# Layer 1 of a four-layer graph network: the scatters of the attention weights in bursts of two and of three, three and two

## The chip, the core and the metric

The kernel runs on one core of a Trainium2 chip. The core has a matrix engine (TensorE, PE in the profile, with its weight loads as PEld), a vector engine (VectorE, DVE), an activation engine (ScalarE, ACT), a general engine (GpSimd, POOL) and SyncE (SP), which here issues most DMA transfers. Each engine runs its own instructions in their order; semaphores hold an instruction until others are done. Scatters with computed rows are DMA transfers that GpSimd issues. The metric is the device time of one execution in microseconds.

## The reference

The input x is 128 graphs of 64 nodes with 256 features, 8192 tokens in all. Four layers follow, each on h = relu(layernorm(x)), each added to x. Layer 1, in which the change lies, is attention over a list of 512 edges:

```python
Xq = (H @ W_lin.T).reshape(bt, n, h, dh)
Xv = (H @ W_val.T).reshape(bt, n, h, dh)
e = einsum('behd,hd->beh', leaky_relu(Xq[:, src] + Xq[:, dst], 0.2), a)
e = e + log(A0[src, dst] + EPS)[None, :, None]
# softmax of e over the edges with the same src: segment_max, exp, segment_sum, division
Y = segment_sum(attn[..., None] * Xv[:, dst], src)
return Y.reshape(bt, n, d) @ W_out.T
```

Layer 0 is two graph convolutions with windows of an LSTM, layer 2 two linear maps with batch normalisation around an aggregation, layer 3 a dense graph attention.

## The kernel before

Tokens go in 16 chunks of 512, and four chunks make a group (0 to 3). Layer 1 has two phases that overlap.

The first is `edges(q)`, 32 times, two blocks of 128 tokens each: queries and values by `project` (L1090), a product that gathers source and target of each edge (L1119), the activation (L1125), the join (L1131), the score of eight blocks gathered in one bank (L1140), at the group's end the linear part (L1156). On GpSimd beside it stand the head sums (L1107), and the roots (L106 to L109) and placed rows (L130) of the next chunks' layer norm. When a group's scores are complete, `edge_softmax(g)` is put on the list `behind`. It is a generator: each `yield` is a place at which it stops, and `step_behind()` takes it one place on. `edges` calls it three times per q, so a group has 24 steps before the next group's scores come. Its steps are the exponent's argument (L1165), two scans for the segment maximum (L1168, L1170), subtraction and exponent (L1174, L1175), two scans for the sum (L1178, L1180), four reciprocals (L1185), a product (L1187), four transposes (L1193), the copy into `attn` (L1208, in the last group L1201 on ScalarE), and eight scatters (L1222). Each scatter writes 128 rows of 64 numbers into a field in HBM, whose other entries are zero; `come_back` (L1247) then loads that field, 2 MB, as the dense attention `dense[g]`.

The second phase is `values_of(n)`, once per chunk: `weigh(n)` has 64 small products of values and attention (L1320, the "small products") and one copy to SBUF (L1330, yT); then comes what `behind` has to do, the loads for chunk n + 2 (values L1272, residual L1293), `turn_attention` (L1302, two att copies from dense, on ScalarE and VectorE), the store of an earlier chunk (L1425), and `put_out` of the chunk before (L1342, the output product, and two additions L1352 that release its PSUM banks). Last come `sums`, the layer-norm statistics for layer 2 (L1362, L1365 on VectorE; x_rs and x_nm, L1367 to L1372, on GpSimd). Sums of chunks 2 to 5 are held and paid from chunk 7 on, two per chunk. Chunks 0 to 3 run within the last eight `edges`, chunks 4 to 15 behind them.

The last group's scores are ready at chunk 3. Its softmax runs beside chunks 3 to 6 and must give `dense[3]` for chunk 12 (`LAST`). In this group each scatter also waits for the last small product issued so far (`last_weigh`, by `add_manual_dep`), and `come_back` is issued within chunk 9. In the kernel before, chunk 6 takes it through the transposes and `attn`, and chunk 7 calls `finish_behind()`, which issues all eight scatters behind chunk 7's small products, so its `yield` after five scatters has no effect.

The order of instructions on an engine follows the program, except where a scheduler may move one; `late(...)` marks those that it must keep in program order. The PSUM banks are a ring of four (`bank`) and of two pairs (`pair`).

Of the kernel before, what the change touches and what calls it, by code (L numbers as in the profile page):

```python
# [31 lines left out]
def gnn_stack_kernel(ctx: ExitStack, tc: tile.TileContext, a: dict, out: bass.AP):  # L32
# [3 lines left out]
    NGR = NTOK // GROUP  # L36
# [7 lines left out]
    def bank():  # L44
        return psums["now"].tile([P, 512], F32, tag="bank", name="bank", bufs=psums["banks"])
# [32 lines left out]
    def late(ins):  # L78

        tc.keep_in_program_order(ins)  # L80
# [398 lines left out]
    with ExitStack() as l0:  # L479
# [451 lines left out]
        for slot in range(len(tasks) + 2):  # L931
# [26 lines left out]
            if new:  # L958
# [8 lines left out]
                if step.w == MAX_SKIP and step.t == 2 and k < 2 and step.g < NGR - 1:  # L967
                    for u in range(2):
                        n = 4 * step.g + 2 * u + k
                        later.append((slot, "x", n))  # L970
            while later and later[0][0] <= slot:
                _, kind, n = later.pop(0)
# [27 lines left out]
    with ExitStack() as l1:  # L1000
# [32 lines left out]
        for g, c, u, ip in last_outs:  # L1033
            if not ip:
                n = 4 * g + 2 * u + c
# [126 lines left out]
        def edge_softmax(g):  # L1162

            e = e1.tile([P, E], F32, tag="e", name="e")
            late(nc.vector.scalar_tensor_tensor(e, scores[g], 0.8, logw, ALU.mult, ALU.add))  # L1165
            run = e1.tile([P, E], F32, tag="run", name="run")
            yield
            late(nc.vector.tensor_tensor_scan(run, first, e, NEG, ALU.add, ALU.max))  # L1168
            yield
            late(nc.vector.tensor_tensor_scan(  # L1170
                run[:, ::-1], final[:, ::-1], run[:, ::-1], NEG, ALU.add, ALU.max
            ))
            yield
            late(nc.vector.tensor_tensor(e, e, run, ALU.subtract))  # L1174
            late(nc.scalar.activation(e, e, AF.Exp))  # L1175
            yield

            late(nc.vector.tensor_tensor_scan(run, keep, e, 0.0, ALU.mult, ALU.add))  # L1178
            yield
            late(nc.vector.tensor_tensor_scan(  # L1180
                run[:, ::-1], final[:, ::-1], run[:, ::-1], NEG, ALU.add, ALU.max
            ))
            yield
            for k in range(NE):
                late(nc.vector.reciprocal(run[:, k * P : (k + 1) * P], run[:, k * P : (k + 1) * P]))  # L1185
                yield
            late(nc.vector.tensor_tensor(e, e, run, ALU.mult))  # L1187
            yield
            for _ in range(2 if g < NGR - 1 else 0):
                yield  # L1190
            p = bank()
            for ec in range(NE):
                ins = nc.tensor.transpose(p[:, ec * P : (ec + 1) * P], e[:, ec * P : (ec + 1) * P], ident)  # L1193
                if ec == 0:
                    late(ins)
            if g < NGR - 1:
                yield
            attn = e1.tile([P, E], F32, tag="run", name="attn").rearrange("p (e r) -> p e r", e=NE)
            if g == NGR - 1:
                for ec in range(NE):  # L1200
                    late(nc.scalar.activation(  # L1201
                        attn[:, ec, :],
                        p[:, ec * P : (ec + 1) * P],
                        AF.Identity,
                        scale=twins[:, ec : ec + 1],
                    ))
            else:
                late(nc.vector.tensor_tensor(  # L1208
                    attn,
                    p.rearrange("p (e r) -> p e r", e=NE),  # L1210
                    twins.unsqueeze(2).to_broadcast([P, NE, P]),
                    ALU.mult,
                ))

            sent = []

            dense[g] = attp.tile([P, T, T], F32, tag="dense", name="dense")
            if g == NGR - 1:
                yield
            for par in range(2):  # L1220
                for ec in range(NE):
                    ins = nc.gpsimd.indirect_dma_start(  # L1222
                        out=fields1[g][:, :],
                        out_offset=bass.IndirectOffsetOnAxis(ap=row_of[:, par, ec : ec + 1], axis=0),
                        in_=attn[:, ec, par * T : (par + 1) * T],
                        in_offset=None,
                    )
                    if g < NGR - 1:
                        late(ins)
                    for earlier in sent:  # L1230
                        tc.declare_no_dep(ins.ins, earlier.ins, reason="different rows")
                    sent.append(ins)
                    if g == NGR - 1:

                        tc.add_manual_dep(
                            ins.ins,
                            last_weigh[0].ins.name,
                            mybir.DependencyInfo(mybir.DependencyClass.Sync, mybir.DependencyReason.DATA),
                            reason="weights first",
                        )  # L1240
                        if len(sent) == 5:
                            yield
                    else:
                        yield
            def come_back():

                back = nc.sync.dma_start(  # L1247
                    out=dense[g].rearrange("p s r -> p (s r)"),
                    in_=fields1[g][: 2 * T * T, :].rearrange("(p s) r -> p (s r)", p=P),
                )  # L1250
                if g == NGR - 1:
                    late(back)
                for ins in sent:
                    tc.add_manual_dep(
                        back.ins,
                        ins.ins.name,
                        mybir.DependencyInfo(mybir.DependencyClass.Sync, mybir.DependencyReason.DATA),
                        reason="rows of the field",
                    )

            if g < NGR - 1:
                come_back()
            else:
                last_back.append(come_back)
# [44 lines left out]
        def weigh(n):  # L1309

            xv, att = fetched.pop(n), turned.pop(n)
            yT = yp.tile([P, 8, 2, T], F32, tag="yT", name="yT")
            p = pair_bank()
            for c in range(2):
                for i in range(4):
                    for h2 in range(2):
                        for par in range(2):
                            r = slice(par * T, (par + 1) * T)
                            hd = 2 * c + h2
                            ins = nc.tensor.matmul(  # L1320
                                p[h2 * T : (h2 + 1) * T, par, (c * 4 + i) * T : (c * 4 + i + 1) * T],
                                xv[r, i, hd * T : (hd + 1) * T],
                                att[r, i % 2, i // 2 * 4 + hd, :],
                                start=True,
                                stop=True,
                            )
                            if c + i + h2 + par == 0:
                                late(ins)
            last_weigh[0] = ins
            nc.scalar.copy(  # L1330
                yT.rearrange("p k o t -> p o k t"), p.rearrange("p o (k t) -> p o k t", t=T)
            )
            return (yT,)
# [42 lines left out]
        def step_behind():  # L1376

            while behind:
                try:
                    next(behind[0])  # L1380
                    return
                except StopIteration:
                    behind.pop(0)

        def finish_behind():
            while behind:
                step_behind()
# [8 lines left out]
        def values_of(n, hold=False):  # L1396

            one = (n, *weigh(n))
            if n == 6:
                step_behind()  # L1400
            elif n == 7:
                finish_behind()
            if n + 2 < NCH:
                fetch(n + 2)
            if n == LAST:
                turn_attention(n + 1)
            if n + 2 < NCH and not LAST <= n + 2 < LAST + 2:
                turn_attention(n + 2)
            flush_stores()
            flush_values()  # L1410
            if n == 5:
                step_behind()

            if n + 1 == LAST:
                turn_attention(LAST)
            weighed.append(one)
            if not hold:
                for _ in range(2 if n > 6 else 4):
                    if unnormed:
                        sums(*unnormed.pop(0), 7 <= n < 11)  # L1420

        def flush_stores():
            while stores:
                m, xt = stores.pop()
                nc.sync.dma_start(out=xb[m], in_=xt)  # L1425

        def flush_values():
            if weighed:
                put_out(*weighed.pop())
# [110 lines left out]
    with ExitStack() as l2:  # L1540
# [55 lines left out]
        with ExitStack() as dense2:  # L1596
# [67 lines left out]
            with ExitStack() as first_dense:  # L1664
# [43 lines left out]
                for slot, (pr, m2) in enumerate(tasks):  # L1708
                    n = slot + 3
# [542 lines left out]
```

## Time and profile before

| | |
|---|---|
| median of three timed runs | 1955.58 us (1952.48 to 1955.93) |
| profiled execution | 1963.28 us, span 1961.5 us |
| TensorE busy | 1918.5 us, 98% of the span |
| VectorE, ScalarE, GpSimd busy | 1329.9, 1161.9 and 458.2 us |
| scatters (L1222) | 32, 34.9 us in all, the first at 1369.6 us, the last at 1546.0 us |
| small products (L1320) | 1024, from 1459.5 us on |
| mean granted clock of TensorE | 0.997 |

A timeline row gives the start and the length in us, engine, line, operation, tiles and count; in brackets the idle time before it and what ended it, where "issue" stands for nothing that the profile shows. The slices on the page are 49 us each. A row of stages has the stretch, its length, the busy time of PE, PEld, DVE, ACT and POOL (with instructions), the granted clock, the DMA engines' busy share and GB/s.

### The profile page before, as it was taken

Reading aid. Unit: us, or ns where it says so; the run is one execution under the profiler, and the core shown is the slowest. Engines: PE = TensorE matmul, PEld = TensorE weight load, DVE = VectorE, ACT = ScalarE, POOL = GpSimd, SP = SyncE. Lnnn points to the kernel's source line nnn. Section 1 sums busy time; section 2 is a strip of 40 time slices with the busy share of each in tenths; the row PEclk is TensorE's granted clock in tenths of the full one; section 3 lists DMA queues with packets and bytes.
Section 4 is the critical chain, followed back from the end, with each engine's and each line's share of the span. In section 5 each row is a group of like instructions: output and inputs, shape, how many; then the busy total and the mean of one; then the engine's idle time right before and its main releaser. Section 6 shows DMA issues by size and latency. Waiting matters only on the chain. (4 is left out here: it accounts for less than half of the span.)

```text
span 1961.5 us, 25191 instructions
## 1 busy us (share of the span) xinstructions
PE 1918.5 (98%) x9150; PEld 1395.5 (71%) x9150; DVE 1329.9 (68%) x2506; ACT 1161.9 (59%) x2169; POOL 458.2 (23%) x614
## 2 busy tenths in 40 slices
PE   9999999999999999999999999999999899999998
PEld 7777478866678874788666788876666775534787
DVE  8774675574475567765754655678887677787887
ACT  4353775564565547665654656587776456592554
POOL 3000031040030011320400200265675420000574
PEclk9999999999999999999999999999999899999999
DMA  7512000010010044000100100441334741022112
GB/s 268 177 60 97 0 22 1 1 44 0 1 43 1 1 161 140 22 1 0 44 0 1 43 1 17 142 159 66 123 124 162 279 156 60 1 65 86 44 65 87
DMA packets 63868, 135.57 MB, mean 69 GB/s; under 512 B 6656, under 2 KB 41344, under 8 KB 61440
## 3 DMA queue, kind: packets, MB, share of 16 engines
q1 hardware_dynamic: 59808, 124.33, 18.6%
q0 software_dynamic: 3328, 9.44, 1.2%
q8 instruction: 72, 1.18, 0.3%
q14 instruction: 52, 0.43, 0.1%
q10 hardware_dynamic: 608, 0.20, 0.0%
HBM read 87.55 MB, written 46.40 MB: 68 GB/s over the span
## 5 line engine op out<-in xcount | busy, mean ns | idle before, releaser
L767 ACT ACTIVATE gate<-gate,bias 128x256 f32<-128x256 f32 (+2 forms) x368 | 247.4, 679 | 175.0 <-DVE gate L783 92.7
L739 PE MATMUL pa<-xop,sih 128*128 128x256 f32 (+2 forms) x1056 | 342.4, 417 | 5.3 <-DVE gate L793 4.1
L739 PEld LDWEIGHTS pa<-xop,sih 128*128 128x128 f32 x1056 | 198.5, 190 | 76.1 <-issue 19.1
L739 PE MATMUL pc<-xop,wih 128*128 128x256 f32 (+2 forms) x736 | 251.2, 423 | 0.0
L783 DVE TENSOR_TENSOR gate<-pb,gate 128x256 f32<-128x256 f32 (+2 forms) x184 | 87.6, 476 | 226.3 <-PE pb L739 155.4
L739 PE MATMUL pa<-lstm_h,shh 128*128 128x256 f32 (+1 forms) x672 | 212.7, 398 | 0.0
L739 PEld LDWEIGHTS pc<-xop,wih 128*128 128x128 f32 x736 | 139.8, 190 | 51.2 <-issue 22.5
L800 DVE TENSOR_TENSOR gate<-pc,gate 128x256 f32<-128x256 f32 (+2 forms) x184 | 87.7, 476 | 112.2 <-PE pc L739 111.7
L1125 ACT ACTIVATE lr<-pair 128x1024 f32<-128x1024 f32 x128 | 124.4, 1025 | 48.4 <-PE pair L1119 19.5
L739 PEld LDWEIGHTS pa<-lstm_h,shh 128*128 128x128 f32 x672 | 127.7, 190 | 30.2
L739 PE MATMUL pc<-lstm_h,whh 128*128 128x256 f32 (+1 forms) x448 | 141.8, 398 | 0.0
L782 ACT COPY gate<-pa 128x256 f32<-128x256 f32 (+2 forms) x184 | 76.0, 413 | 87.1 <-PE pa L739 86.6
L1090 PE MATMUL bank<-wlv,hT 128*128 128x260 f32 x480 | 117.1, 384 | 8.6 <-DVE xq L1101 4.8
L793 DVE TENSOR_TENSOR gate<-pa,gate 128x256 f32<-128x256 f32 (+2 forms) x184 | 87.5, 475 | 41.4 <-PE pa L739 40.7
L767 ACT ACTIVATE gate<-pa,bias 128x256 f32<-128x256 f32 (+2 forms) x184 | 93.8, 510 | 30.7 <-PE pa L739 28.8
L787 ACT COPY gate<-pa 128x256 f32<-128x256 f32 (+2 forms) x184 | 75.1, 408 | 57.9 <-PE pa L739 56.8
L1090 PEld LDWEIGHTS bank<-wlv,hT 128*128 128x128 f32 x480 | 87.6, 190 | 25.5 <-DVE xq L1101 7.2
L739 PE MATMUL pa<-xop,wih 128*128 128x256 f32 (+1 forms) x320 | 101.7, 399 | 1.3 <-ACT xop L718 1.2
L739 PE MATMUL pb<-xop,wih 128*128 128x256 f32 (+1 forms) x320 | 100.7, 398 | 0.4 <-POOL xop L718 0.4
L739 PEld LDWEIGHTS pc<-lstm_h,whh 128*128 128x128 f32 x448 | 85.1, 190 | 20.1
L506 POOL TENSOR_TENSOR shh<-whh 128x512 f32<-128x512 f32 x6 | 7.6, 1273 | 381.9 <-PE pa L739 245.7
L790 ACT COPY gate<-pc 128x256 f32<-128x256 f32 (+2 forms) x136 | 57.8, 425 | 53.4 <-PE pc L739 52.8
(376 smaller groups left out, 4021.9 us busy)
## 6 DMA issues: line engine op xcount, KB each, us to landing
field<-keep SPq DMA_DIRECT2D x4, 2304.0 KB
wih<-in_WihT SPq DMA_DIRECT2D x8, 1024.0 KB, 6.9
xres<-in_x SPq DMA_DIRECT2D x16, 512.0 KB
xa<-xres POOLq DMA_DIRECT2D x16, 512.0 KB
dense<-field SPq DMA_DIRECT2D x4, 2048.0 KB
xin<-xb SPq DMA_DIRECT2D x16, 512.0 KB, 3.7
h<-xb SPq DMA_DIRECT2D x16, 512.0 KB, 3.6
xin<-in_x SPq DMA_DIRECT2D x15, 512.0 KB, 6.9
```

Source lines behind the costliest of these rows:

```text
L506: keep(nc.gpsimd.tensor_tensor(o, x, y, op))
L739: ins = nc.tensor.matmul(p[:, : self.N], weights[kind, self.phase](k, q), x[k], start=first_ and kind == "ih", stop=kind == "hh" or not se ...
L767: nc.scalar.activation(out, in_, AF.Tanh if q == 2 else AF.Sigmoid, bias=bias[:, self.w - 1, 2 * q + j : 2 * q + j + 1],)
L782: nc.scalar.copy(blk[0, 0], pa[:, :N])
L783: nc.vector.tensor_tensor(blk[0, 0], pb[:, :N], blk[0, 0], ALU.add)
L787: nc.scalar.copy(blk[1, 0], pa[:, :N])
L790: (nc.vector.tensor_copy if not self.t and self.w > 1 else nc.scalar.copy)(blk[1, 1], pc[:, :N])
L793: nc.vector.tensor_tensor(blk[1, 1], pa[:, :N], blk[1, 1], ALU.add)
L800: nc.vector.tensor_tensor(blk[1, 0], pc[:, :N], blk[1, 0], ALU.add)
L1090: ins = nc.tensor.matmul(o, hTs[n][:, k, i * P : (i + 1) * P], wlv[:, k, cols], start=k == 0, stop=k == 1)
L1125: nc.scalar.activation(lr, p, AF.Relu)
```

## The change

```diff
                             reason="weights first",
                         )
-                        if len(sent) == 5:
-                            yield
-                    else:
+                    if len(sent) in ((3, 6) if g == NGR - 1 else (2, 4, 6, 8)):
                         yield
...
             one = (n, *weigh(n))
-            if n == 6:
+            if n in (6, 7):
                 step_behind()
-            elif n == 7:
+            elif n == 8:
                 finish_behind()
```

In groups 0 to 2 a step now issues two scatters instead of one, so such a group needs 19 steps and not 23, and the dense load follows earlier. Group 2's four spare steps go to group 3, which has therefore taken four steps instead of three when chunk 3 begins and is through its product L1187 when chunk 4 does. Chunk 5's step is now the transposes and `attn`; the step in chunk 6 issues scatters 1 to 3 behind that chunk's small products, the one in chunk 7 scatters 4 to 6, and `finish_behind()` in chunk 8 the last two. On TensorE only the four transposes of the last group change place: they stand ahead of chunk 6's small products instead of behind them. On ScalarE the last group's exponent stands ahead of the att copies of chunk 5, and its `attn` copies ahead of chunk 6's yT copy. On GpSimd scatters 4 to 6 of groups 0 and 1 come ahead of the roots, and one chunk's x_rs and x_nm stand between scatters 6 and 7 of the last group. On SyncE the dense loads of groups 0 and 1 come ahead of one or two other loads, and the load of chunk 12's residual ahead of the last dense load.

## The prediction

> **What bounds the kernel now.** I read the page first, then one stage of the trace. The page's first part and its clock row:
>
> ```profile
> PE 1918.5 (98%) x9150; PEld 1395.5 (71%) x9150; DVE 1329.9 (68%) x2506; ACT 1161.9 (59%) x2169; POOL 458.2 (23%) x614
> ...
> PEclk9999999999999999999999999999999899999999
> ```
>
> TensorE is busy for 98% of the span, so a microsecond counts only if TensorE loses or gains it. The one slice in which its granted clock is below full is the 32nd, 1520 to 1569 us: the tail of layer 1, where the changed instructions stand. TensorE's timeline there:
>
> ```profile
> 1515.42 1.16 PE L1320 MATMUL pair<-att,xv_in 64*64 64x64 f32 x64
> 1520.16 1.16 PE L1320 MATMUL pair<-att,xv_in 64*64 64x64 f32 x64
> ...
> 1531.24 0.63 PE L1193 MATMUL bank<-ident,e 128*128 128x128 f32 x4 [0.43 <-DVE e L1187]
> ...
> 1535.25 1.16 PE L1320 MATMUL pair<-att,xv_in 64*64 64x64 f32 x64
> ...
> 1540.00 0.98 PE L1320 MATMUL pair<-att,xv_in 64*64 64x64 f32 x44
> 1541.39 0.30 PE L1320 MATMUL pair<-att,xv_in 64*64 64x64 f32 x3 [0.41 <-issue]
> ...
> 1547.09 0.35 PE L1320 MATMUL pair<-att,xv_in 64*64 64x64 f32 x1 [0.45 <-issue]
> ...
> 1548.97 6.34 PE L1342 MATMUL bank<-wout,yT 128*128 128x256 f32 x16
> 1555.25 1.16 PE L1320 MATMUL pair<-att,xv_in 64*64 64x64 f32 x64
> ```
>
> L1320 is a chunk's 64 small products, L1342 the output product of the chunk before. A chunk takes 4.74 us (1515.42 to 1520.16). Chunk 8, from 1540.00, is the exception: 44 products run at full pace, and the last 20 take until 1548.97, one per 0.71 us with "issue" as the reason, so no semaphore that the trace shows. GpSimd at that time (its timeline, first and last of the eight scatters of the last group):
>
> ```profile
> 1537.19 0.96 POOL L1222 DMA_INDIRECT field<-attn,row_of  x1 [24.52 <-issue]
> ...
> 1540.98 0.96 POOL L1222 DMA_INDIRECT field<-attn,row_of  x1 [0.30 <-issue]
> ...
> 1546.04 0.96 POOL L1222 DMA_INDIRECT field<-attn,row_of  x1 [0.30 <-issue]
> ```
>
> The slow pace begins as the fourth scatter starts and ends 1.5 us after the eighth. The queues of 1541 to 1548.1 us, and the stages (span; PE, PEld, DVE, ACT, POOL busy; clock; DMA share; GB/s):
>
> ```profile
> q0 software_dynamic: 256, 0.26, 10.6%
> ```
> ```profile
> 1535.20:1540.00 4.80, 4.80 (x82) 3.99 (x81) 1.90 (x3) 1.99 (x2) 2.20 (x3) 1.00 1.03 413
> 1541.00:1545.30 4.30, 1.44 (x8) 0.71 (x8) 3.31 (x15) 0.00 (x0) 3.38 (x4) 0.86 0.61 232
> 1545.30:1549.00 3.70, 1.70 (x13) 0.95 (x13) 0.00 (x0) 0.00 (x0) 3.07 (x6) 0.50 0.08 29
> 1549.00:1555.20 6.20, 6.20 (x19) 4.79 (x16) 0.85 (x3) 1.98 (x2) 4.47 (x9) 0.57 0.87 312
> 1555.20:1560.00 4.80, 4.80 (x83) 3.99 (x82) 4.65 (x17) 1.99 (x2) 2.72 (x6) 1.00 0.89 309
> ```
>
> q0 carries the scatters. All 256 packets of the eight (32 each) move between 1541 and 1548.1; in 1536 to 1541 q0 does not appear, since q1's loads fill the DMA engines. So the products are slow exactly while scatter packets move. The clock is 0.86 in 1541 to 1545.3, that is half from about 1544.1, 3.1 us after the slow pace began, and the next output product takes 6.34 us instead of 3.72. Chunk 8 to chunk 9 is 15.25 us instead of 4.74: **10.5 us lost**, the largest stall of TensorE within the kernel.
>
> **The change, part by part.** Durations are of the profiled execution (1963.28 us, span 1961.5), which is 7.7 us above the median of the timed runs (1955.58). I sum against it and take the difference to the median.
>
> 1. *Group 2 ends earlier, group 3's softmax starts one step earlier.* Two scatters per place take four steps off groups 0 to 2, so the last group's steps shift by one: its exponent moves ahead of the att copies of chunk 5 on ScalarE, its four transposes (L1193) ahead of chunk 6's small products. Now they cost 5.60 − 4.74 = 0.86 us between chunks 6 and 7, of which 0.43 is a wait for L1187. Replaying VectorE's new order with its durations (second scan ends 1518.74, subtract 0.66, two output additions 0.66 each, two scans 1.23, four reciprocals 0.85, one addition) puts L1187's end at 1529.2 to 1529.6; the product ahead of the transposes ends at 1529.65. Bounds: −0.43 (no wait) to +0.3. I take −0.1.
>
> 2. *The burst of eight becomes 3 + 3 + 2.* Scatters 1-3 wait for chunk 6's products (end about 1531.3), 4-6 for chunk 7's, 7 and 8 for chunk 8's. A scatter's pitch is 1.26 us, the first starts 0.8 us after the products' end (1536.41 to 1537.19), so a burst of three is issued from +0.8 to +4.3 us, and the next products begin at +3.6. They overlap the third scatter's issue. In the trace of before the 44 fast products ran beside just that (third scatter 1539.72 to 1540.67) and lost nothing. What matters is when the packets move. Lag from issue to movement: 4.0 us with full DMA queues (1537.19 to 1541.2), and about 1.9 us in the quieter group 2. With 4 us the first burst's packets move at 1536.3 to 1539.8, between chunk 7's products (1535.0 to 1536.1) and chunk 8's (1539.7); the second's at 1541 to 1544, between chunks 8 and 9 (1544.4). With 1.9 us they hit chunk 7's products, which then wait until the packets are through, about 2 us a burst. Bounds for the new halts: 0 to 6 us. DMA share is 1.03 there now, so I stand near the long lag: +0.7. Removed: −10.5.
>
> 3. *Behind the third burst.* GpSimd's order now has one chunk's four x_rs/x_nm instructions (L1367 to L1372, 1.97 us) between scatters 6 and 7; they wait for VectorE's sums, done about 1542, so scatters 7 and 8 go at 1544.3 to 1546.5. SyncE waits for them to load dense (L1247, now issued at 1549.70 behind the load of chunk 11's values, which waits for the slow products). New: about 1548 to 1550; the same load of group 0 took some 6.5 us, so it lands at 1554.5 to 1557. Its readers are chunk 12's two att copies on ScalarE, due after chunk 11's yT copy, at about 1556. Bounds 0 to +1; taken 0, since VectorE is later still (next). The store of chunk 7 (L1425) waits behind this load on SyncE; nobody reads it before layer 2. The load of chunk 12's residual moves ahead of it.
>
> 4. *VectorE loses its pause.* It owes two chunks' sums per chunk from 7 to 10: 8 x (0.39 + 0.17) = 4.5 us, two output additions 1.38, an att copy 0.58, some 6.4 us per 4.74. In the trace it stood idle for 8.5 us of the stall and was then full (4.65 of 4.80). Without the stall it falls behind by up to 4 x 1.7 = 6.7 us; the output products' banks allow 7.6 (two chunks less half a product), but chunk 13's att copy stands behind chunk 10's addition. The replay gives chunk 13 a wait of 1.2 us. Bounds 0 to 2.5; taken +1.2.
>
> 5. *Groups 0 and 1.* Scatters 4-6 come 3 to 10 us earlier, in a burst of 3.8 us ahead of the roots (L106 to L109) and placed rows (L130). These rows are read some 9 us later (placed by 1381.0, transposed at 1389.95), the head sums by the linear product at the group's end. On SyncE dense moves ahead of xin: xin 0 would go at about 1388 instead of 1383.64 and land by 1396, its first reader is at 1399.17. Group 2 already has a burst of six, with TensorE busy for 13.89 of 15.00 us beside it. Zero; if that cover were gone, a late xin would cost up to 3 us per group.
>
> Sum: −10.5 − 0.1 + 0.7 + 1.2 = **−8.7 us**: 1954.6 against the profile's own time, **1946.9** on the scale of the median.
>
> The trace's row is the slow products while scatters move, gone with scatters out of the way. [...] I keep to the row: nothing else was active from 1545.3 to 1549.
>
> **The rivals.**
>
> *B, short lag.* Packets meet the products three times. Each halt is about 2 us, short of the 3.1 after which the clock fell: 3 x 2 = 6 instead of 0.7, 1952.2. For it: lag 1.9 us in group 2. Against: DMA share 1.03.
>
> *C, no halt to remove in the timed runs.* The profile is 7.7 us above the median, and the stall with no semaphore could belong to the profiled execution. Then only the small terms stay: 1955 to 1957. For it: that gap, and a reason "issue". Against: an identical burst in group 2 is not disturbed, so it isn't a constant price of the recording.
>
> *D, slower: each burst halts the next products until its last packet lands and the clock falls.* A halt is then about 4 us (the lag of 4.0 us, behind products that begin as the third scatter is issued), past the 3.1 us of the clock, and half clock costs some 1 us of the 2.6 that it cost now, three times: 15 us − 10.5 + 0.3 = +5, about 1960. It decides from 3.5 us per burst. For it: each third scatter overlaps products and DMA is full. Against: 44 products ran at full pace.
>
> **How the numbers follow.** A (the sum) 0.44, B 0.16, C 0.14, D 0.26. About 0.2% (3.9 us) is what a measurement of this kernel can tell. Faster: A and three quarters of B, 0.56. Same: the rest of B and most of C, 0.14. Slower: D and a little of C, 0.30. A alone spans 1943.5 (no new halt, no late VectorE, no late transposes) to 1951. The range needs part of D: 1943.5 to 1961.
>
> **What the profile after would show.** Chunk 8 to chunk 9 at about 4.8 us; scatters in three groups with 1.3 us pitch; full clock in 1545 to 1555; 1.2 us before chunk 13's products put down to VectorE. Wrong: "issue" pauses in the products of chunk 7, 8 or 9 (B, D), or an unchanged total with the stall gone (C). What would make me wrong most simply is a lag between issue and packets other than 4 us.

## The result, and the profile after

The changed kernel took 1962.72 us (1961.57 to 1967.74, six runs) beside 1954.61 us (1952.48 to 1955.93, six runs) of the kernel before: 1.0048 times as long, 95% interval 1.0034 to 1.0062. It is slower by 8.1 us; 1946.9 had been predicted. Its profiled execution took 1964.65 us and is one of its six runs. The one of before took 1963.28 us, is not among the six of that kernel and lies over 7 us above the slowest of them, so it may come from another occasion than the timed runs.

The page of the changed kernel, TensorE's line and its clock row:

```profile
PE 1919.1 (98%) x9150; PEld 1396.3 (71%) x9150; DVE 1328.8 (68%) x2506; ACT 1162.4 (59%) x2169; POOL 458.4 (23%) x614
...
PEclk9999999999999999999999999999999999999999
```

The 8 in the clock row is gone, and yet TensorE is no less busy (half clock of 3.41 and 6.83 us, as below, does not show in slices of 49 us). TensorE's timeline in the tail of layer 1 (line numbers from here on are two lower than in the kernel before: L1318 are the small products, L1340 the output product, L1300 the att copies):

```profile
1543.03 1.16 PE L1318 MATMUL pair<-att,xv_in 64*64 64x64 f32 x64
...
1547.78 1.16 PE L1318 MATMUL pair<-att,xv_in 64*64 64x64 f32 x64
...
1552.52 1.16 PE L1318 MATMUL pair<-att,xv_in 64*64 64x64 f32 x64
...
1562.00 1.16 PE L1318 MATMUL pair<-att,xv_in 64*64 64x64 f32 x64
...
1568.45 0.34 PE L1318 MATMUL pair<-att,xv 64*64 64x64 f32 x8 [1.63 <-ACT att L1300]
1569.42 1.77 PE L1318 MATMUL pair<-att,xv 64*64 64x64 f32 x56 [0.63 <-ACT att L1300]
1571.12 4.55 PE L1340 MATMUL bank<-wout,yT 128*128 128x256 f32 x16
1575.60 1.16 PE L1318 MATMUL pair<-att,xv 64*64 64x64 f32 x64
```

Chunks 7, 8 and 9 (the first three rows) run at full pace, 4.74 us apart: the stall of before is gone, as forecast. Chunk 12 (1568.45) comes 6.4 us after chunk 11 (1562.00) instead of 4.74, because ScalarE waits for the dense load:

```profile
1567.33 2.03 ACT L1300 COPY att<-dense 128x512 f32<-128x512 f32 x2 [3.03 <-DMA dense<-field]
```

Chunk 13 comes another 7.2 us later: the products wait once more (0.63 us), and half clock, granted from 1569.43 for 3.41 us, does the rest. But most of the loss lies earlier. TensorE in group 1, before and after:

```profile
1444.35 1.20 PE L1119 MATMUL pair<-sd_hot,xq 128*128 128x512 f32 x4
1445.38 0.60 PE L173 MATMUL bank<-ident,h 128*128 128x128 f32 x4
1445.82 1.91 PE L1090 MATMUL bank<-wlv,hT 128*128 128x260 f32 x8
1447.37 1.43 PE L1119 MATMUL pair<-sd_hot,xq 128*128 128x512 f32 x4
```
```profile
1446.69 1.20 PE L1119 MATMUL pair<-sd_hot,xq 128*128 128x512 f32 x4
1451.02 1.24 PE L173 MATMUL bank<-ident,h 128*128 128x128 f32 x4 [3.12 <-POOL h L130]
1452.05 3.65 PE L1090 MATMUL bank<-wlv,hT 128*128 128x260 f32 x8
1455.14 2.04 PE L1119 MATMUL pair<-sd_hot,xq 128*128 128x512 f32 x4
```

The transposes L173 wait 3.12 us for the placed rows L130 of GpSimd, and the products behind them take nearly twice their time. The stages of the changed kernel (stretch, length, busy time of PE, PEld, DVE, ACT, POOL, clock, DMA share, GB/s) show that the clock is half in that stretch:

```profile
1447.90:1451.00 3.10, 0.00 (x0) 0.00 (x0) 2.56 (x7) 2.47 (x3) 2.90 (x5) 0.83 0.04 13
1451.00:1456.80 5.80, 5.78 (x16) 4.50 (x17) 2.03 (x3) 1.40 (x3) 4.02 (x7) 0.50 0.34 90
```

The account between the two traces, from how far each instruction of TensorE is behind its own place in the trace of before: 0.7 us behind ahead of group 0; 2.4 after group 0's transposes (their wait is 1.15 us); 8.4 after group 1 (3.1 of wait and 2.9 of half clock); 8.2 at chunk 3. The first 0.7 us are not the change's: the changed kernel was 0.9 us ahead until a half clock of 3.41 us from 1361.2, before any scatter. So groups 0 and 1 cost 7.7 us in this trace. Then −0.4 for the transposes, −10.5 for the stall, +1.7 and +2.4 at chunks 12 and 13: 1.4 us behind at chunk 15 (1585.09 against 1583.70). So trace against trace the changed kernel is 1.4 us slower, by the medians of the timed runs 8.1 us. That gap became the second question.

### The profile page after: what moved, and what is told of

Read it like the earlier page. It is cut to its first block, busy times and chain, and to the rows that moved or that the text cites. A ratio compares the mean times of both kernels' runs of the same rounds, so it can differ in the third digit from the quotient of the medians.

```text
span 1962.9 us, 25193 instructions
## 1 busy us (share of the span) xinstructions
PE 1919.1 (98%) x9150; PEld 1396.3 (71%) x9150; DVE 1328.8 (68%) x2506; ACT 1162.4 (59%) x2169; POOL 458.4 (23%) x614
```

## The experiments

In each, the kernel of comparison is the kernel before, run on the same chip. Three chips took part; the time of before was 1960.6 to 1970.3 us on all of them, in 72 executions, while it had been 1952.5 to 1955.9 us where the change was measured. No chip is named for that first measurement: that it was a fourth one, and not one of these three at another time, is an inference. "The chip of the measurement" below stands for it.

**The two halves of the change apart.** The tail alone leaves groups 0 to 2 at one scatter per place and gives the list one more step ahead of chunk 3, so that the last group's softmax stands where the changed kernel has it. In its profile lines are numbered as in the kernel before.

```diff
-                        if len(sent) == 5:
+                        if len(sent) in (3, 6):
                             yield
...
-            for _ in range(4 if last_one else 0):
+            for _ in range(5 if last_one else 0):
...
-            if n == 6:
+            if n in (6, 7):
                 step_behind()
-            elif n == 7:
+            elif n == 8:
                 finish_behind()
```

> Groups 0 to 2 as in the kernel before (one scatter per place); only the last group in 3 + 3 + 2, with its softmax one step early as in the changed kernel. Theory 1 (the timed runs of before have no 10.5 us stall in chunk 8's products, so the tail's part returns nothing and pays for the dense load that comes late for chunks 12 and 13, 1.7 + 2.4 us in the trace of after): 1954.6 - 0.4 + 4.1 = about 1958, ratio 1.000 to 1.003. Theory 2 (the stall is in the timed runs too, and groups 0 and 1 lose more than the 8.2 us of the trace): 1954.6 - 10.5 + 3.7 = about 1948, ratio 0.996 to 0.997. In the trace, both: no pause in chunks 7 to 9, no wait of L173 for L130, chunk 12 after chunk 11 by about 6.4 us.

The groups alone:

```diff
-                    else:
+                    elif len(sent) in (2, 4, 6, 8):
                         yield
...
-            for _ in range(4 if last_one else 0):
+            for _ in range(3 if last_one else 0):
```

> Groups 0 to 2 two scatters per place as in the changed kernel; the last group as in before, all eight behind chunk 7. Theory 1 (the loss is that of groups 0 and 1, 8.2 us in the trace of after): 1954.6 + 8.2 = about 1963, ratio 1.003 to 1.005, and a trace in which L173 waits for L130 in groups 0 and 1, and the stall of chunk 8's products is absent or, if present, goes with a time some 8 us above this kernel's median. Theory 2 (stall in the timed runs, groups lose more): 1962.7 + 10.5 - 3.7 = about 1969.5, ratio 1.007 to 1.008, with the stall in the trace.

The tail alone took 1954.11 us, before 1963.15: ratio 0.9960 (0.9946 to 0.9974), 9.0 us faster. The groups alone took 1972.29: ratio 1.0048 (1.0031 to 1.0066), 9.1 us slower. On this chip theory 1 is wrong about the tail and theory 2 about the size of the loss in groups 0 and 1: the stall is in the timed runs here, the tail's part returns most of it, and groups 0 and 1 cost 9.1 us, near the 7.7 of the trace. With them ran the kernel before itself.

> The kernel before once more, for a second profile. If the stall of chunk 8's products belongs to single executions, this one may show chunk 8 to chunk 9 at 4.7 us and a time near 1954; if it is in every execution, 15 us again and a time near 1954 as well or, if profiled executions are slower, near 1963.

1962.72 us, and the stall is there. Chunks 8 and 9 in this second profile of before:

```profile
1539.92 0.99 PE L1320 MATMUL pair<-att,xv_in 64*64 64x64 f32 x44
...
1554.76 1.16 PE L1320 MATMUL pair<-att,xv_in 64*64 64x64 f32 x64
```

14.84 us instead of 4.74. The tail alone, chunks 7 to 9:

```profile
1534.06 0.96 PE L1320 MATMUL pair<-att,xv_in 64*64 64x64 f32 x44
1535.40 0.59 PE L1320 MATMUL pair<-att,xv_in 64*64 64x64 f32 x20 [0.39 <-issue]
...
1539.58 0.98 PE L1320 MATMUL pair<-att,xv_in 64*64 64x64 f32 x44
1540.94 0.58 PE L1320 MATMUL pair<-att,xv_in 64*64 64x64 f32 x20 [0.38 <-issue]
...
1545.11 1.24 PE L1320 MATMUL pair<-att,xv_in 64*64 64x64 f32 x46
1546.72 0.54 PE L1320 MATMUL pair<-att,xv_in 64*64 64x64 f32 x18 [0.37 <-issue]
```

The expectation of no pause failed: after each burst the next chunk's products stop once, again after 44 to 46 of 64. But each stop costs only 0.8, 0.8 and 1.0 us (the last behind the burst of two), so 2.6 us stand in place of 10.1, and the dense load is not late then (chunk 12 follows chunk 11 after 4.74 us).

**Two bursts of four.**

```diff
-                        if len(sent) == 5:
+                        if len(sent) == 4:
                             yield
...
-            for _ in range(4 if last_one else 0):
+            for _ in range(5 if last_one else 0):
```

> As the kernel with the tail alone, but the last group's scatters in two bursts of four, behind chunks 6 and 7, so that no x_rs instruction stands ahead of one and the dense load goes out some 5 us earlier. Theory (the late dense load costs chunks 12 and 13 about 4 us): 3 to 4 us below the kernel with 3 + 3 + 2, chunk 12 after chunk 11 by at most 5 us: 1954 if the stall is not in the timed runs, 1944 to 1945 if it is. Rival (VectorE's sums hold chunks 12 and 13, so an earlier load gives nothing): within 1 us of the kernel with 3 + 3 + 2.

1956.08 us, ratio 0.9965 (0.9953 to 0.9977): 2 us above the tail alone, so neither expectation. The dense load was not late there, so there was nothing to gain from an earlier one, and the stops grew:

```profile
1534.95 0.94 PE L1320 MATMUL pair<-att,xv_in 64*64 64x64 f32 x43
1536.30 0.35 PE L1320 MATMUL pair<-att,xv_in 64*64 64x64 f32 x4 [0.41 <-issue]
...
1541.81 1.25 PE L1320 MATMUL pair<-att,xv_in 64*64 64x64 f32 x44
```

Chunk 7 to chunk 8 is 6.86 us, chunk 8 to chunk 9 6.51: the stops cost 3.9 us together, 1.3 more than the tail alone's. The other 0.7 us are within the spread of the tail alone's four timings (1954.1 to 1955.4). A burst of two or three costs 0.8 to 1.0 us here, one of four 1.8 to 2.1, one of eight 10.1, of which half clock in the output product behind it makes 2.2 (5.94 instead of 3.72 us): from three to eight more than in proportion.

**How many scatters stand ahead of the roots.** If groups 0 and 1 lose because placed rows come late, the loss must follow the number of scatters that GpSimd takes ahead of the roots. The two kernels are the tail alone with one and with two places saved in each of groups 0 and 1 (four in the changed kernel); in GpSimd's order one and two more scatters then stand ahead of the roots (three more in the changed kernel). For one more ahead:

```diff
-                    else:
+                    elif g == 2 or len(sent) in (1, 2, 3, 4, 5, 6, 8):
                         yield
```

and, for two more ahead:

```diff
-                    else:
+                    elif g == 2 or len(sent) in (1, 2, 3, 4, 6, 8):
                         yield
```

> As the kernel with the tail alone, but in groups 0 and 1 only scatters 7 and 8 share a place; in GpSimd's order one more scatter then stands ahead of the roots of each of these groups (three more in the changed kernel). Theory (a scatter ahead of the roots moves the placed rows by its pitch of 1.26 us, against a slack of 0.98 us before the transposes): a wait of about 0.3 us in each group, 0.6 us above the kernel with the tail alone, that is about 1954.7, L173 waiting for L130 by 0.2 to 0.5 us twice. Rival (the loss comes with the number of places saved, by the loads that the dense load passes on SyncE): one place of four saved, 2 us above, 1956.

> As before, with two more scatters ahead of the roots in groups 0 and 1 (scatters 5 and 6, 7 and 8 share a place). Theory (slack): 2 x 1.26 - 0.98 = 1.5 us of wait in each group, 3.0 us, and up to 1.7 us more for each pause after which the clock falls to half for 3.4 us: 1957 to 1960.5. Rival (places saved): two of four, 4.3 us, 1958.4, with the wait on something else than L130.

> The changed kernel once more, beside the kernel before. The kernel before took 1954.6 us where the change was measured and 1963.15 us where the first four runs were made, with the 10.5 us stall in its profile there; the changed kernel took 1962.7. Theory (the stall of the kernel before comes and goes with the chip; the changed kernel has none, and pays 8.6 us in groups 0 and 1): if before is near 1963 here, the changed kernel is at 1962 to 1964, ratio 0.999 to 1.001; if before is near 1954.6, 1962.7 again, ratio 1.004. Rival (the whole chip runs 0.4% slower and the stall is in both): the changed kernel at 1970.6 beside a before of 1963, ratio 1.004 in both cases.

One more: 1955.33 us, ratio 0.9965 (0.9953 to 0.9978), and no wait of L173 for L130 in its trace. Two more: 1957.98 us, 0.9979 (0.9969 to 0.9988). The changed kernel beside them: 1963.47 us, 0.9998 (0.9989 to 1.0008). Their waits (engine, line and whom for; us in total, times, longest), two more and then three:

```profile
PE bank L173 <- POOL h L130: 2.3, 2, 1.1
```
```profile
PE bank L173 <- POOL h L130: 5.7, 2, 3.1
```

From the first scatter of group 1 to the end of the first placed row it is 10.89 us in the kernel before, and 10.96, 13.66 and 15.66 us with one, two and three more scatters ahead; the wait is 0, 0, 1.14 and 3.12 us. So a row that ends 2.77 us later is waited for by 1.14, one that ends 4.77 us later by 3.12: both times the slack was 1.6 us. One more scatter costs nothing because the row ends hardly later: it starts 1.15 us later (10.41 us behind the first scatter instead of 9.26), but takes 0.55 us to place instead of 1.63, which the expectation had not allowed for; why is not shown. The rival (each place saved costs the same, 2.1 us) fits two places in time (1958.4), but not the wait, which is on L130, nor the other steps: one place saved cost nothing in the trace (the 1 us in the timing is within the spread of the tail alone, which was not run beside it), two about 4 us, and the last step, in which the wait is followed by half clock, over 5 of the 9 in all. GpSimd's order in the changed kernel, group 1, shows the step. The kernel before has three scatters ahead of L106, the last of them being the first row here; the changed one has six.

```profile
1436.45 0.96 POOL L1222 DMA_INDIRECT field<-attn,row_of  x1 [0.31 <-issue]
...
1437.71 1.30 POOL L106 TENSOR_SCALAR ln_rs<-ln_mv 128x4 f32<-128x4 f32 x1
...
1442.22 2.18 POOL L130 TENSOR_SCALAR h<-xin,ln_rs,ln_nm 128x256 f32<-128x256 f32 x2
```
```profile
1438.79 0.96 POOL L1222 DMA_INDIRECT field<-attn,row_of  x1 [0.30 <-issue]
...
1440.12 1.99 POOL L1222 DMA_INDIRECT field<-attn,row_of  x1 [0.17 <-issue]
1442.42 0.95 POOL L1222 DMA_INDIRECT field<-attn,row_of  x1 [0.30 <-issue]
1443.67 0.96 POOL L1222 DMA_INDIRECT field<-attn,row_of  x1 [0.30 <-issue]
1444.71 1.06 POOL L106 TENSOR_SCALAR ln_rs<-ln_mv 128x4 f32<-128x4 f32 x1
...
1448.52 1.08 POOL L1222 DMA_INDIRECT field<-attn,row_of  x1 [0.18 <-issue]
...
1450.08 1.43 POOL L130 TENSOR_SCALAR h<-xin,ln_rs,ln_nm 128x256 f32<-128x256 f32 x2
```

The changed kernel on that chip answers the second question in part: it takes there what it took where it was measured, 1963, and it is the kernel before that is 8 us slower. Its tail is not the same, though. Chunks 7 and 8 there:

```profile
1543.63 0.85 PE L1318 MATMUL pair<-att,xv_in 64*64 64x64 f32 x41
1545.03 0.61 PE L1318 MATMUL pair<-att,xv_in 64*64 64x64 f32 x23 [0.56 <-issue]
...
1549.22 1.01 PE L1318 MATMUL pair<-att,xv_in 64*64 64x64 f32 x44
1550.62 0.59 PE L1318 MATMUL pair<-att,xv_in 64*64 64x64 f32 x20 [0.39 <-issue]
```

Here the products stop behind each burst; in the first profile, of the same program on the chip where the change was measured, the same products run through.

**Scatters moved off the small products.** As the tail alone, but the scatters of the last group wait for the first product of the output product that follows, and their step comes behind that output product instead of ahead of it.

```diff
-                            last_weigh[0].ins.name,
+                            first_out[0].ins.name,
...
                         if i + c == 0:
                             late(ins)
+                            first_out[0] = ins
...
-            if n in (6, 7):
-                step_behind()
-            elif n == 8:
-                finish_behind()
...
-            if n == 5:
+            if n in (5, 6, 7):
                 step_behind()
+            elif n == 8:
+                finish_behind()
```

> As the kernel with the tail alone, but each scatter of the last group waits for the first product of the output product that follows the small products, and no longer for the last small product; scatters start some 0.3 us later. Theory (the small products pause only when scatter packets begin to move while they are being issued; in the kernel with the tail alone the first packets moved at 1535.0 and the products stopped at 1535.02, in the changed kernel they moved 0.3 us after the products and none stopped): no pause, 2.6 us less, about 1951.5 where the kernel with the tail alone takes 1954.1. Rival (a burst costs TensorE its 0.8 us wherever it lies): 1954, with pauses of 0.4 us of reason issue again.

1956.13 us, ratio 0.9970 (0.9958 to 0.9983): the theory falls. Chunk 7 stops twice:

```profile
1535.48 0.92 PE L1320 MATMUL pair<-att,xv_in 64*64 64x64 f32 x44
1536.79 0.35 PE L1320 MATMUL pair<-att,xv_in 64*64 64x64 f32 x5 [0.40 <-issue]
1537.54 0.49 PE L1320 MATMUL pair<-att,xv_in 64*64 64x64 f32 x15 [0.39 <-issue]
```

The products stop at 1536.40, while the first packet of the burst moves after 1537.5. The stop comes 0.9 us after the products begin and not when packets begin; the burst before it is what all stops share. The expectation had misread the tail alone, too: its first packet moves at 1535.50, half a microsecond after the products stop (1535.02). In all 16 profiles with stops the first one comes before the first packet of the burst, by 0.1 to 1.4 us; in the prediction's own trace they are 1540.98 and 1541.22. So packets that begin to move do not start the stops. Another rival, instructions that reach TensorE late, was not tested. The trace of before speaks against it: the two packets of its instruction queues in the slow stretch start at 1543.3 and 1544.3 us and take 0.95 and 0.5 us, and the products stay slow until 1548.5.

**In search of an execution of before near 1954.6 us.** The kernel before was profiled three more times, the tail alone was timed three more times, and the groups alone once.

> The kernel before, a third profile. If it takes near 1963: the stall of 10.5 us between chunks 8 and 9 again. If it takes near 1954.6: chunk 9 follows chunk 8 after 5 to 7 us, clock full, and the rest of layer 1 as in the other profiles within 1 us.

> Groups 0 to 2 as before, the last group in 3 + 3 + 2, once more and with more rounds. Theory (the gain is the stall): ratio 0.995 to 0.997 where before takes near 1963; where before takes near 1954.6 and has no stall, no pauses here either, but the dense load late for chunks 12 and 13 (4.1 us in the first trace of the changed kernel): 1954 to 1958, ratio 1.000 to 1.002.

> The kernel before, one more profile, in search of an execution near 1954.6. Where it takes that: chunk 9 follows chunk 8 after 5 to 7 us. Where it takes 1963: 15 us as in the four profiles so far.

> The tail alone once more. Where before takes near 1963: ratio 0.995 to 0.997. Where it takes near 1954.6: 1954 to 1958, ratio 1.000 to 1.002.

> The kernel before, one more profile. Where it takes near 1954.6: chunk 9 follows chunk 8 after 5 to 7 us. Where it takes 1963: 15 us.

> The tail alone. Where before takes near 1963: ratio 0.995 to 0.997. Where it takes near 1954.6: 1954 to 1958, ratio 1.000 to 1.002.

> Groups 0 to 2 two scatters per place, the last group as before, once more. Where before takes near 1963: ratio 1.004 to 1.006, the stall in the profile (chunk 9 after chunk 8 by 15 us). Where before takes near 1954.6: 1962 to 1964, ratio 1.004 to 1.005, and no stall in the profile (chunk 9 after chunk 8 by at most 7 us).

None was found. Before took 1965.25, 1965.45 and 1966.64 us in these profiles, with 14.7, 14.7 and 14.9 us from chunk 8 to chunk 9. The tail alone: 1954.08 us, ratio 0.9953 (0.9939 to 0.9967); 1954.15 us, 0.9955 (0.9940 to 0.9970); 1955.38 us, 0.9963 (0.9952 to 0.9974). The groups alone: 1970.73 us, 1.0033 (1.0016 to 1.0051). The last is a little under what was expected (1.004). So on three chips the stall is in all four profiles of the kernel before taken there, as in the one given with it, the tail's part gains 6.5 to 9.9 us (by medians), and groups 0 and 1 take 6.3 and 9.1 us away. That the stall is missing where before takes 1954.6 us is not shown. For it speaks that the changed kernel's profile from that very chip has no stop behind its bursts. It also fits that the profile of before is slower than any timed run of its kernel and as slow as those three chips are. Without the stall, the terms of the trace give 8.2 − 0.4 + 4.1 = 11.9 us slower (0.7 of them from before group 0); 8.1 was measured. Of the remaining 3.8 us, 1.9 is that the profiled execution lay above its median; the rest is open.

## Why the prediction was wrong

- **Groups 0 and 1 (part 5), taken as zero: the step that failed.** It set the end of the placed rows (1381.0) against transposes at 1389.95, a cover of 9 us. The transposes that read these rows are those at 1381.98; the ones at 1389.95 read the two rows placed later. The cover was 0.98 us by that row, which ends with the second of the two placed; the first, which the first transposes read, ends at 1380.45, and by the runs the slack is 1.6 us. Three scatters of 1.26 us ahead of the roots are 3.8 us, and the row ended 4.8 us later in group 1, more than any of these. The price was 7.7 us in the trace, 7.9 to 10.9 in the three other profiles with this order, and 9.1 and 6.3 us in the two timings of the groups alone. Where the prediction asks what a lost cover would cost, it names the wrong reader, a late xin; the rows' reader was the one that waited, and the half clock behind the wait (2.9 us of the 6.0 in group 1, half of the 5.8 us in its stage row) was not in the sum.
- **The removed stall, −10.5.** Right by its size on the three chips (14.84 − 4.74 = 10.1 in the second profile). In the runs that measured the change it most likely did not exist; that is argued, not shown. This error was needed too for a slower kernel: where the stall was there to remove, the change comes out level (1963.47 us beside 1962.88). The prediction had seen the sign, a profile 7.7 us above the median, and left this to rival C with 0.14 because group 2's burst disturbed nothing. That argument was weak: group 2's burst stands beside large products. The gap between the profile and the median should have weighed more: 7.7 us, most of the stall's size.
- **New halts (part 2), +0.7.** 2.6 us on the three chips (between forecast and rival B), 0 on the chip of the measurement. The cause that the term rests on, packets that move beside the products, is not what the profiles show: the first stop comes before the first packet.
- **The transposes (part 1), −0.1.** −0.4, the lower bound: no wait for L1187.
- **The dense load (part 3), 0.** In the first profile it was late: issued at 1557.98, which is 1549.8 without the 8.2 us by which all was late, so within the forecast; but ScalarE could read it only 9.3 us later (1567.33), where 6.5 had been taken from group 0's load. That is 1.7 us at chunk 12 and 2.4 at chunk 13, the latter mostly half clock. Where products stop behind each burst it costs 0 to 0.6 us.
- **VectorE's lag (part 4), +1.2.** Not seen: chunk 13 follows after 4.74 us in the tail alone.

Parts 1 to 4 sum to −8.7 in the prediction; the tail alone, which is parts 1 to 4, measured −9.0 us in its first timing. That is partly luck: by the profiles the terms were −10.1, −0.4, +2.6 and 0, together −7.9, with the halts too small in the forecast and VectorE's lag too large, and the four timings lie from −6.5 to −9.9. The lower end of the range, 1943.5, does not come out of its parts either: 1955.58 − 10.5 − 0.43 is 1944.7. Of the rivals, C is the one that the measured comparison fits for the tail; D, which stood for "slower", did not happen anywhere: no burst of three halted products for over 1.4 us, and D needed 3.5. The slower result came from a mechanism that no rival named. On the chip of the measurement, in its one profile, no products stopped (chunks 7 to 10 begin 4.74 us apart); on three chips they stopped behind every burst of the last group, but there the first stop came before a packet moved, so these runs do not show that it is the DMA.

The best of the kernels here is the tail alone: 1954.1 us where both the kernel before and the changed one take 1963. It wasn't run on the chip where before takes 1954.6.

## What to carry to other kernels

Where an edit puts more work ahead of something on an engine that is only a quarter busy, find for each product of that engine the very instruction that reads it, by tile and by which part of the tile, and take the slack from the tightest such pair; a reader one instance too late made a slack of 1.6 us look like 9 here. Add to a wait of TensorE the half clock that can follow: 2.9 us behind a wait of 3.1 here. And when a profiled execution lies above all timed ones by most of the stall that an edit is to remove, measure the kernel on several chips before counting on it.

## What the runs showed of the hardware that was not expected

- One program, unchanged, took 1954.6 us in the measurement of the change and 1963 on three chips (72 executions, none below 1960.6), while another that differs in the order of scatters took 1963 both times. That the chip makes the difference is likely, not shown.
- Products of 64 x 64 stop after 41 to 48 of 64 in the chunk behind a burst of indirect scatters, on those three chips, wherever the burst's packets are. Where there are several they come mostly 0.7 or 1.4 us apart, and their cost rises faster than the burst: 0.8 to 1.1 us for two or three scatters (up to 1.4 in the kernel with the later scatters), 1.8 to 2.1 for four, 10.0 to 10.5 for eight, the last with half clock. The cause stays open.
- At the transposes L173 of groups 0 and 1, a wait of TensorE of 1.1 to 1.2 us was not followed by half clock (three cases), one of 2.5 us in one of three, one of 3.1 us in all four. The length of a wait does not decide alone: one of 1.6 us (chunk 12 of the changed kernel) was followed by it, and so were, in six of the 17 profiles, two waits of 1.0 and 0.9 us with 1.1 us between them, near 1425 us, which all 17 have. The half clock of 3.41 us from 1361.2 in the changed kernel cost 1.6 us.
- Half clock was granted for 3.41 us (in the changed kernel from 1361.2 and from 1569.43), 6.83 us (in its group 1 from 1450.0, 2.1 us after TensorE's last product) and 10.24 us (in the kernel before from 1544.1): one, two and three times 3.41.
